# A graph layer's group loop: sums copied by VectorE, carries read from PSUM

## The chip, the cores and the metric

The kernel runs on one core of a Trainium2 chip. A core has five engines with instruction queues of their own: TensorE (matmuls and transposes; PE and PEld in the profile), VectorE (DVE), ScalarE (ACT), GpSimd (POOL) and SyncE (SP). TensorE writes its results to PSUM; the other data on the chip lies in SBUF. The metric is the time of one execution in microseconds (us) on the device; the time given for a kernel is the median of its runs.

## The reference

One layer of graph attention with 12,500 nodes of 128 features and 200,000 edges that are sorted by their destination. It has 4 heads of 32 columns. Cut to what matters:

```python
h = relu(layernorm(x)) @ W_node.T                    # one row for every node
att = leaky(sum([h[src], h[dst], edge @ W_edge.T] * a), 0.2)   # edge x head
m  = max(segment_max(att, dst), 0)                   # node x head
ex = exp(att - m[dst])
den = segment_sum(ex, dst) + (E - degree) * exp(-m)
out = x + segment_sum(ex / den[dst] * h[src], dst)
```

The softmax is taken over all edges, so that the E - degree edges that do not end at a node each add exp(-m) to its denominator.

## The kernel before

**Tiling.** Edges are cut into 392 groups of 511 (`NE`), with one slot ahead of them for a carry, so that a group is 512 slots: 4 columns (`J`) of 128. Four groups are a quad; there are 98 quads. Quads are gathered into super groups of 2, 2, then 4 each, and 2, 2, 1, 1 at the end; a super group shares one softmax. As destinations are sorted, the edges of a group end within a window of 96 nodes (`WIN`), whose first node is a number in the tile `base`.

**Prologue.** GpSimd starts at once to gather the raw rows of the source nodes of quads 0 to 3. Meanwhile TensorE computes a table row of 137 numbers for every node (4 heads of 32 values and a one, a count of one, 4 source terms) and writes it to `table` in HBM. From quad 4 on, GpSimd gathers from `table`: `gather` (L126) issues one indirect DMA of 128 rows for each column, 16 a quad, 1502 in all (L135). The gathered rows of a quad lie in one of eight `ga` buffers. Quads 0 to 3 hold raw rows and are turned into table rows on the core by `converted` (L235); for quads 2 and 3 that is called as `late(2)` and `late(3)` in the main loop, with ScalarE copying from PSUM.

**Main loop.** The order of the work is written out by hand (`tc.manual_schedule()`): every engine runs its instructions in the order in which the program issues them. `together` takes several generators and issues one step of each in turn. In the main loop the generators are these:

- `all_logits(q)` first calls `flush`, which adds up the logits of the quad before it with `add_sources` (L508; L519 is the first to read the gathered rows of that quad). Then it calls for the transfers of quad q + 2, by `fetch`, and computes the logits of its own four groups (L497 on VectorE, L502 and L505 on TensorE).
- `softmax(s)` (L530) transposes the logits of a super group to one row for each group and head, takes the leaky slope (L546 on ScalarE, L549 on VectorE), scans for the maxima of each segment, with what comes in from the group before, and takes exp(att - maximum) (L587). It turns three things back to the layout of edges: the exponentials (L598, in the bank `ex_ps`), a factor for each group's carry (L590, L595, L603, copied to `facs` by L605), and the maximum of each segment, stored at its last edge (L592, L608, copied to `xs` by L610). It has five steps.
- `sums(q)` (L646) prepares the quad: it copies the last-edge flags to column 96 of `hot` (L657) and the maxima to `ga` (L659, one for each group), both on ScalarE. For each group it multiplies the gathered values by the exponentials (L663), makes a one-hot matrix of the destinations (L666) and lets TensorE add up columns 1 to 3 into a PSUM bank `acc` (L671). Then it calls `complete()`, which ends the group before.
- `complete_group` (L627) ends a group. Row 96 of a group's sums is the part of a node that goes on in the next group. VectorE scales it into the carry's slot in column 0 of `ga` (L632), ScalarE copies the count (L636), TensorE adds column 0 (L637), and ScalarE copies the 97 x 137 sums to SBUF, `pt` (L638). After the last group of a quad ScalarE takes exp(-maximum) for the denominators (L642).
- `divide` (L676) divides a quad's sums on VectorE (L681 to L689), adds x (L692), and SyncE writes four windows of 96 rows (L694). Windows overlap, so each write waits for the one before it.

**Buffers and queues.** A `ga` buffer comes free when L637 of the quad's last group has run; GpSimd's gathers of the quad eight later wait for that. The `acc` banks are three in number, and are used by `late` as well. SyncE's queue carries the loads of edge features (`ea`), destinations (`db`), windows of `side` and x (`pw`, `xw`), the destination rows of a super group (`dr`), and the writes. A window's first node is loaded into one of SyncE's registers by `window(g)` (L454), once for `pw` and `xw` and once more for the write. `checked` (L716) tests in small steps, from the sixth super group on, that the destinations are sorted and fit their windows; its four loads of `rows` are issued by ScalarE.

**Main loop's order.** For a super group s of quads q0 and on: the last quad of the super group before is summed in one `together` with the first `all_logits` ahead and `softmax(s)`; then each but the last quad of s is summed beside one `all_logits` of the next super group; then the logits that are left follow. After the first super group, `complete()` and `late(3)` come in between.

Of the kernel before, what the change touches and what calls it, by code (L numbers as in the profile page):

```python
# [8 lines left out]
F32 = mybir.dt.float32  # L9
BF16 = mybir.dt.bfloat16  # L10
I32 = mybir.dt.int32
AF = mybir.ActivationFunctionType
OP = mybir.AluOpType
AX = mybir.AxisListType

P = 128
# [5 lines left out]
LN2 = 0.6931471805599453  # L22

# [3 lines left out]
J = 4  # L27
# [18 lines left out]
def kernel(  # L46
# [388 lines left out]
    with tc.tile_pool(name="work", bufs=2) as work, \  # L435
# [18 lines left out]
        def window(g):  # L454
            return nc.values_load(
                base[0:1, g:g + 1], engines=[mybir.EngineType.SP], min_val=0, max_val=N - 1,
                skip_runtime_bounds_check_because="a destination, which is a node")

        def fetch_windows(q):
# [3 lines left out]
            at = [window(g0 + i) for i in range(m)]  # L463
# [66 lines left out]
        def softmax(s):  # L530
# [14 lines left out]
            low = turned.tile([SBG * H, NE], F32, name="low")  # L545
            nc.scalar.mul(low[:R], t_ps[:R, 1:GE], SLOPE)  # L546
            yield
            att = t_ps[:R, 1:GE]
            nc.vector.tensor_tensor(att, att, low[:R], op=OP.max)  # L549
# [12 lines left out]
            for h in range(H):  # L562
# [13 lines left out]
            top = turned.tile([SBG * H, NE], F32, name="top")  # L576
# [6 lines left out]
                                         op0=OP.mult, op1=OP.max)  # L583
            ex = turned.tile([SBG * H, GE], F32, name="ex")
            nc.vector.memset(ex[:R, 0:1], 0.0)
            nc.vector.tensor_tensor(ex[:R, 1:GE], att, top[:R], op=OP.subtract)
            nc.scalar.activation(ex[:R, 1:GE], ex[:R, 1:GE], AF.Exp)  # L587

            fac = turned.tile([SBG * H, 1], F32, name="fac")
            nc.scalar.activation(fac[:R], top[:R, 0:1], AF.Exp, bias=col[:R], scale=-1.0)  # L590

            nc.vector.scalar_tensor_tensor(run_e, same_next, 0.0, top[:R],  # L592
                                           op0=OP.is_equal, op1=OP.mult)
            diag = turned.tile([SBG * H, SBG * H], F32, name="diag")
            nc.vector.tensor_scalar(diag[:R, :R], ident[:R, :R], fac[:R], None, op0=OP.mult)  # L595
            yield
# [3 lines left out]

            other = acc_pool.tile([P, 512], F32, name="acc")
            fac_ps = other[:, 0:R]
            nc.tensor.matmul(fac_ps, ones[:R, :], diag[:R, :R], start=True, stop=True)  # L603
            facs = turned.tile([P, SBG * H], F32, name="facs", bufs=2)
            nc.scalar.copy(facs[:, :R], fac_ps)  # L605
            top_ps = other[:, 512 - J * SBG * H:].rearrange("p (j r) -> p j r", j=J)[:, :, 0:R]
            for j in range(J):
                nc.tensor.transpose(top_ps[:, j, :], run[:R, j * P:(j + 1) * P], ident[:R, :R])  # L608
            xs = turned.tile([P, J, SBG * H], F32, name="xs", bufs=2)
            nc.scalar.copy(xs[:, :, 0:R], top_ps)  # L610
            XS[s] = ex_ps[:, 0:J * SBG * H].rearrange("p (j r) -> p j r", j=J), xs, facs
# [4 lines left out]
        begun = []  # L616
        state = {}

        def complete():

            division = state.pop("division", None)
            if begun:
                complete_group(*begun.pop())
            if division:
                divide(*division)

        def complete_group(q, i, ga, hot, pt, acc, fc):  # L627
            g0, m = quads[q]
            g = g0 + i
            if g:  # L630
                before = state["before"]
# [4 lines left out]
                nc.scalar.copy(ga[0:1, i, 0, R_CNT:R_CNT + 1], before[WIN:WIN + 1, R_CNT:R_CNT + 1])  # L636
            nc.tensor.matmul(acc, hot[:, i, 0, :], ga[:, i, 0, :], start=False, stop=True)  # L637
            nc.scalar.copy(pt[:, i, :], acc)  # L638
            state["before"] = pt[:, i, :]
            if i == m - 1:  # L640
                den = work.tile([WIN, QG, H], F32, name="den")
                nc.scalar.activation(den[:, :m, :], pt[0:WIN, :m, R_SRC:R_SRC + H], AF.Exp,  # L642
                                     scale=-1.0)
                state["division"] = q, pt, den

        def sums(q):  # L646
# [6 lines left out]
            ex, xs, facs = XS[s]  # L653
# [3 lines left out]
            nc.scalar.copy(hot[:, :m, :, WIN], is_last[:, g0:g0 + m, :])  # L657
            for i in range(m):
                nc.scalar.copy(ga[:, i, :, R_SRC:R_SRC + H], heads(xs)[:, :, :, g0 - s0 + i])  # L659
# [328 lines left out]
```

## Time and profile before

| what | us |
|---|---|
| median of 3 runs | 2074.68 |
| lowest, highest | 2072.62, 2075.88 |
| the profiled execution | 2940.07 |
| its span, first to last instruction | 2938.3 |
| TensorE busy (matmuls) | 1385.1 |
| VectorE busy | 1363.1 |
| ScalarE busy | 427.3 |
| GpSimd busy | 1489.6 |

The profile is of one execution, which took longer than the runs that were timed. Rows of the page and of the answers name a line of the kernel, its engine, its operation and the tiles that it writes and reads; busy time and waits are in us, the mean of one instruction in ns. In a timeline the columns are the start, the duration, the instruction, how many were merged, and in square brackets the idle time of the engine ahead of it with what ended it. "remote" is a wait whose end the profile can't put down to an instruction. The mean granted clock of TensorE was 0.537 of full speed.

### The profile page before, as it was taken

The numbers are of one execution on the slowest core, as the hardware profiler recorded it, in microseconds if no ns is written. First come the engines' busy times: TensorE is split into PE (matmuls) and PEld (weight loads), VectorE is DVE, ScalarE is ACT, GpSimd is POOL, SyncE is SP. The second block draws the span as 40 slices with busy tenths as digits, with TensorE's granted clock in tenths as the row PEclk, the third lists the DMA queues.
The fourth block names the chain that finished last, engine by engine and source line by source line (L and its number), as shares of the span: only waits on it lengthen the run. The fifth ranks groups of instructions, "written<-read, shape, count | busy, mean of one in ns | idle before, by whom it ended". The sixth has DMA issues, their size and how long they took to land.

```text
span 2938.3 us, 29033 instructions
## 1 busy us (share of the span) xinstructions
PE 1385.1 (47%) x7275; PEld 1254.9 (43%) x7275; DVE 1363.1 (46%) x3314; ACT 427.3 (15%) x1766; POOL 1489.6 (51%) x1574
## 2 busy tenths in 40 slices
PE   1524644444445444454454454454454454454465
PEld 1424544444444444444344344344343443444354
DVE  1614444444444444454454454454454454454476
ACT  1523111111111111111111111111111111111111
POOL 7062345555555555555555555555555555555510
PEclk9955555555555555555555555555555555555556
DMA  4333344444444444444444444444444444444320
GB/s 139 124 101 80 85 122 104 100 110 103 100 110 99 110 111 103 99 115 104 99 111 103 102 109 100 106 108 99 106 104 102 109 103 102 110 99 107 92 68 15
DMA packets 214494, 299.10 MB, mean 102 GB/s; under 512 B 86122, under 2 KB 162154, under 8 KB 204915
## 3 DMA queue, kind: packets, MB, share of 16 engines
q1 hardware_dynamic: 162512, 184.97, 23.3%
q0 software_dynamic: 50112, 109.65, 17.3%
q10 hardware_dynamic: 1698, 2.58, 0.3%
q8 instruction: 61, 1.00, 0.1%
q14 instruction: 111, 0.90, 0.1%
HBM read 270.49 MB, written 26.52 MB: 101 GB/s over the span
## 4 chain that ended last, share of the span: by engine, by line
another core or an unknown queue 43%; PE 21%; DVE 14%; issue 10%; ACT 4%; DMA 1%; SPq 1%; ACTq 0%; DVEq 0%
PE acc L671 11%; PE lg L505 4%; PE acc L637 3%; DVE at L497 2%; ACT pt L638 1%; DVE run L575 1%; DVE res L689 1%; DVE res L692 1%; DVE ga L632 1%; DVE hot L666 1%; DVE ga L663 1%; PE lg L502 1%; DVE top L581 1%; PE acc L608 1%
## 5 line engine op out<-in xcount | busy, mean ns | idle before, releaser
L135 POOL DMA_INDIRECT ga<-table,srci x1502 | 1428.1, 951 | 1299.9 <-PE acc L637 774.2
L671 PE MATMUL acc<-ga,hot 128*97 128x137 f32 x2352 | 649.2, 448 | 839.8 <-ACT ga L659 747.4
L671 PEld LDWEIGHTS acc<-ga,hot 128*97 128x97 f32 x2352 | 518.5, 279 | 866.3 <-ACT ga L659 758.0
L632 DVE TENSOR_TENSOR ga<-pt,facs 1x132 f32<-1x132 f32 x391 | 112.6, 288 | 1153.4 <-ACT pt L638 1012.7
L638 ACT COPY pt<-acc 97x137 f32<-97x137 f32 x392 | 107.1, 273 | 2103.2 <-remote 1408.9
L505 PE MATMUL lg<-wblk,ea 128*128 128x8 f32 x1568 | 409.0, 359 | 0.0
L505 PEld LDWEIGHTS lg<-wblk,ea 128*128 128x128 f32 x1568 | 381.5, 309 | 0.0
L637 PE MATMUL acc<-ga,hot 128*97 128x137 f32 x784 | 260.7, 436 | 222.1 <-ACT ga L636 144.8
L502 PEld LDWEIGHTS <-at 96*128 96x128 bf16 x1568 | 218.3, 166 | 206.2 <-DVE at L497 118.2
L637 PEld LDWEIGHTS acc<-ga,hot 128*97 128x97 f32 x784 | 197.2, 283 | 232.3 <-ACT ga L636 150.8
L663 DVE TENSOR_TENSOR ga<-ga,ex_ps 128x528 f32<-128x528 f32 x392 | 270.4, 690 | 9.0 <-PE ex_ps L598 8.6
L497 DVE TENSOR_TENSOR at<-const_ps,db 96x512 bf16<-96x512 f32 x392 | 267.1, 683 | 8.1 <-DMA db<-in_dst_dram 2.3
L502 PE MATMUL lg<-pw,at 96*128 96x12 bf16 x1568 | 169.9, 181 | 141.0 <-DVE at L497 99.6
L666 DVE TENSOR_TENSOR hot<-const_ps,slot 128x384 f32<-128x384 f32 x392 | 214.0, 546 | 0.0
L372 PE MATMUL row_ps<-wcat,hT 128*128 128x137 f32 x198 | 39.9, 351 | 79.6 <-issue 21.4
L598 PE MATMUL ex_ps<-ident,ex 64*128 64x64 f32 (+2 forms) x112 | 18.6, 314 | 123.8 <-ACT ex L587 123.8
L636 ACT COPY ga<-pt 1x1 f32<-1x1 f32 x391 | 73.6, 188 | 10.6
L135 POOL DMA_INDIRECT ga<-in_x_dram,srci x64 | 60.5, 946 | 20.7 <-issue 19.2
L372 PEld LDWEIGHTS row_ps<-wcat,hT 128*128 128x128 f32 x198 | 33.6, 243 | 86.1 <-ACT row L373 23.5
L692 DVE TENSOR_TENSOR res<-res,xw 96x512 f32<-96x512 f32 x98 | 67.7, 691 | 3.4
L689 DVE TENSOR_TENSOR res<-pt,const_ps 96x512 f32<-96x512 f32 x98 | 66.9, 683 | 3.4
L598 PEld LDWEIGHTS ex_ps<-ident,ex 64*128 64x128 f32 (+2 forms) x112 | 13.8, 208 | 126.8 <-ACT ex L587 126.8
(129 smaller groups left out, 1016.0 us busy)
## 6 DMA issues: line engine op xcount, KB each, us to landing
db<-in_dst_dram SPq DMA_DIRECT2D x98, 768.0 KB
ea<-in_edge_t_dram SPq DMA_DIRECT2D x98, 512.0 KB
ga<-table,srci POOLq DMA_INDIRECT x1502
xw<-in_x_dram SPq DMA_DIRECT2D x392, 48.0 KB
out_dram<-res SPq DMA_DIRECT2D x392, 48.0 KB
pw<-side SPq DMA_DIRECT2D x392, 2.2 KB
table<-row SPq DMA_DIRECT2D x9, 616.5 KB
xt<-in_x_dram SPq DMA_DIRECT2D x9, 576.0 KB
```

Of the source, the lines that this page charges most:

```text
L135: nc.gpsimd.indirect_dma_start(out=ga[:, i, j, 0:width], out_offset=None, in_=rows, in_offset=bass.IndirectOffsetOnAxis(ap=srci[:, g0 + i, ...
L497: nc.vector.tensor_tensor(at[:, i, :], node_ps[0:WIN, g0 + i:g0 + i + 1].to_broadcast([WIN, GE]), db[:, i, :], op=OP.is_equal)
L502: nc.tensor.matmul(lg[:, i, j].rearrange("p k h -> p (k h)"), at[:, i, j * P:(j + 1) * P], sw, start=i + j == 0, stop=False, skip_group_ch ...
L505: nc.tensor.matmul(lg[:, i, 2 * w:2 * w + 2, 0, :], ea[:, i, w, :], wblk, start=False, stop=True, skip_group_check=True)
L632: nc.vector.tensor_tensor(ga[0:1, i, 0, 0:H * HW].rearrange("p (h w) -> p h w", w=HW), before[WIN:WIN + 1, 0:H * HW].rearrange("p (h w) -> ...
L637: nc.tensor.matmul(acc, hot[:, i, 0, :], ga[:, i, 0, :], start=False, stop=True)
L638: nc.scalar.copy(pt[:, i, :], acc)
L663: nc.vector.tensor_tensor(val, val, heads(ex)[:, :, :, g - s0].unsqueeze(3).to_broadcast([P, J, H, HW]), op=OP.mult)
L666: nc.vector.tensor_tensor(hot[:, i, :, 0:WIN], lane_ps.unsqueeze(1).to_broadcast([P, J, WIN]), slot[:, g, :].unsqueeze(2).to_broadcast([P, ...
L671: nc.tensor.matmul(acc, hot[:, i, j, :], ga[:, i, j, :], start=j == 1, stop=False)
L689: nc.vector.tensor_tensor(res[:, :m, :].rearrange("p g (h d) -> p g h d", d=HD), val[:, :, :, 0:HD], share_ps[:, :m, :].unsqueeze(3).to_br ...
L692: nc.vector.tensor_tensor(res[:, :m, :], res[:, :m, :], xw[:, :m, 0:D], op=OP.add)
```

## The change

It takes ScalarE's copies out of the group loop:

- The bank `acc` of a group is copied to `pt` by VectorE, and one `complete()` later than before: a new list `full` holds the group whose sums are in the bank and not yet copied. The carry of the next group is read from that bank, both its values and its count, by VectorE.
- The last-edge flags and the maxima are copied by VectorE, the maxima of all four groups in one instruction, out of PSUM.
- The leaky slope is taken by VectorE.
- In the softmax ScalarE takes exp(-maximum) for every edge ahead of the last-edge mask, so that the sums hold it at each node and the division needs no exp of its own. A node without edges gives zero there, and `TINY` keeps its denominator from being zero. The carry's factor is taken by the first exp as element 0 of `ex`. The softmax has six steps, and its results stay in the `ex_ps` bank.
- SyncE loads the first nodes of four windows by one call in place of four.
- The four loads of `rows` are issued by SyncE, and the end of the kernel calls `complete()` three times.

```diff
-        def window(g):
-            return nc.values_load(
-                base[0:1, g:g + 1], engines=[mybir.EngineType.SP], min_val=0, max_val=N - 1,
+        def windows(q):
+            g0, m = quads[q]
+            return nc.values_load_multi_w_load_instructions(
+                base[0:1, g0:g0 + m], engines=[mybir.EngineType.SP], min_val=0, max_val=N - 1,
...
-            low = turned.tile([SBG * H, NE], F32, name="low")
-            nc.scalar.mul(low[:R], t_ps[:R, 1:GE], SLOPE)
             yield
             att = t_ps[:R, 1:GE]
-            nc.vector.tensor_tensor(att, att, low[:R], op=OP.max)
+            top = turned.tile([SBG * H, NE], F32, name="top")
+            nc.vector.tensor_scalar(top[:R], att, SLOPE, None, op0=OP.mult)
+            nc.vector.tensor_tensor(att, att, top[:R], op=OP.max)
...
-            nc.vector.memset(ex[:R, 0:1], 0.0)
             nc.vector.tensor_tensor(ex[:R, 1:GE], att, top[:R], op=OP.subtract)
-            nc.scalar.activation(ex[:R, 1:GE], ex[:R, 1:GE], AF.Exp)
-            fac = turned.tile([SBG * H, 1], F32, name="fac")
-            nc.scalar.activation(fac[:R], top[:R, 0:1], AF.Exp, bias=col[:R], scale=-1.0)
+            nc.vector.tensor_tensor(ex[:R, 0:1], col[:R], top[:R, 0:1], op=OP.subtract)
+            nc.scalar.activation(ex[:R], ex[:R], AF.Exp)
+            nc.scalar.activation(top[:R], top[:R], AF.Exp, scale=-1.0)
+            yield
+            diag = turned.tile([SBG * H, SBG * H], F32, name="diag")
+            nc.vector.tensor_scalar(diag[:R, :R], ident[:R, :R], ex[:R, 0:1], None, op0=OP.mult)
             nc.vector.scalar_tensor_tensor(run_e, same_next, 0.0, top[:R],
                                            op0=OP.is_equal, op1=OP.mult)
-            diag = turned.tile([SBG * H, SBG * H], F32, name="diag")
-            nc.vector.tensor_scalar(diag[:R, :R], ident[:R, :R], fac[:R], None, op0=OP.mult)
-            yield
             for j in range(J):
                 nc.tensor.transpose(ex_ps[:, j * SBG * H:j * SBG * H + R], ex[:R, j * P:(j + 1) * P],
                                     ident[:R, :R])
-            other = acc_pool.tile([P, 512], F32, name="acc")
             fac_ps = other[:, 0:R]
             nc.tensor.matmul(fac_ps, ones[:R, :], diag[:R, :R], start=True, stop=True)
-            facs = turned.tile([P, SBG * H], F32, name="facs", bufs=2)
-            nc.scalar.copy(facs[:, :R], fac_ps)
-            top_ps = other[:, 512 - J * SBG * H:].rearrange("p (j r) -> p j r", j=J)[:, :, 0:R]
+            yield
+            facs = turned.tile([WIN + 1, SBG * H], F32, name="facs", bufs=2)
+            nc.vector.tensor_copy(facs[WIN:WIN + 1, :R], fac_ps[WIN:WIN + 1, :])
+            top_ps = other.rearrange("p (j r) -> p j r", j=J)[:, :, 0:R]
             for j in range(J):
                 nc.tensor.transpose(top_ps[:, j, :], run[:R, j * P:(j + 1) * P], ident[:R, :R])
-            xs = turned.tile([P, J, SBG * H], F32, name="xs", bufs=2)
-            nc.scalar.copy(xs[:, :, 0:R], top_ps)
...
         def complete():
             division = state.pop("division", None)
+            ready = full.pop() if full else None
             if begun:
-                complete_group(*begun.pop())
+                complete_group(ready[-1] if ready else state.get("before"), *begun.pop())
+            if ready:
+                q, i, pt, acc = ready
+                nc.vector.tensor_copy(pt[:, i, :], acc)
+                state["before"] = pt[:, i, :]
+                if i == quads[q][1] - 1:
+                    state["division"] = q, pt
             if division:
                 divide(*division)
-        def complete_group(q, i, ga, hot, pt, acc, fc):
+        def complete_group(before, q, i, ga, hot, pt, acc, fc):
...
-                nc.scalar.copy(ga[0:1, i, 0, R_CNT:R_CNT + 1], before[WIN:WIN + 1, R_CNT:R_CNT + 1])
+                nc.vector.tensor_copy(ga[0:1, i, 0, R_CNT:R_CNT + 1],
+                                      before[WIN:WIN + 1, R_CNT:R_CNT + 1])
             nc.tensor.matmul(acc, hot[:, i, 0, :], ga[:, i, 0, :], start=False, stop=True)
-            nc.scalar.copy(pt[:, i, :], acc)
-            state["before"] = pt[:, i, :]
-            if i == m - 1:
-                den = work.tile([WIN, QG, H], F32, name="den")
-                nc.scalar.activation(den[:, :m, :], pt[0:WIN, :m, R_SRC:R_SRC + H], AF.Exp,
-                                     scale=-1.0)
-                state["division"] = q, pt, den
+            full.append((q, i, pt, acc))
...
-            nc.scalar.copy(hot[:, :m, :, WIN], is_last[:, g0:g0 + m, :])
-            for i in range(m):
-                nc.scalar.copy(ga[:, i, :, R_SRC:R_SRC + H], heads(xs)[:, :, :, g0 - s0 + i])
+            nc.vector.tensor_copy(hot[:, :m, :, WIN], is_last[:, g0:g0 + m, :])
+            nc.vector.tensor_copy(
+                ga[:, :m, :, R_SRC:R_SRC + H],
+                heads(tops_at)[:, :, :, g0 - s0:g0 - s0 + m].rearrange("p j h g -> p g j h"))
...
-            nc.vector.tensor_tensor(den[:, :m, :], den[:, :m, :],
+            nc.vector.tensor_tensor(den[:, :m, :], pt[0:WIN, :m, R_SRC:R_SRC + H],
                                     others[:, :m].unsqueeze(2).to_broadcast([WIN, m, H]), op=OP.mult)
-            nc.vector.tensor_tensor(den[:, :m, :], den[:, :m, :], val[:, :, :, HD], op=OP.add)
+            nc.vector.scalar_tensor_tensor(den[:, :m, :], val[:, :, :, HD], TINY, den[:, :m, :],
+                                           op0=OP.max, op1=OP.add)
...
-                nc.scalar.dma_start(rows[:n], dst_rows[g0:g0 + n, 0:NE + 1])
+                nc.sync.dma_start(rows[:n], dst_rows[g0:g0 + n, 0:NE + 1])
...
-            complete()
-            complete()
+            for _ in range(3):
+                complete()
```

## The prediction

> **What bounds the kernel now.** I read the page first, then the table of waits, GpSimd's timeline, the timeline of one standstill, and the tail. The page, engines, chain and costliest group:
>
> ```profile
> PE 1385.1 (47%) x7275; PEld 1254.9 (43%) x7275; DVE 1363.1 (46%) x3314; ACT 427.3 (15%) x1766; POOL 1489.6 (51%) x1574
> another core or an unknown queue 43%; PE 21%; DVE 14%; issue 10%; ACT 4%; DMA 1%; SPq 1%; ACTq 0%; DVEq 0%
> L135 POOL DMA_INDIRECT ga<-table,srci x1502 | 1428.1, 951 | 1299.9 <-PE acc L637 774.2
> ```
>
> No engine is full, and 43% of the chain has no name. The waits (us in total, times, longest) put it on ScalarE's copy of the sums:
>
> ```profile
> ACT pt L638 <- remote: 1408.9, 102, 19.1
> DVE ga L632 <- ACT pt L638: 1012.7, 160, 14.6
> POOL ga L135 <- PE acc L637: 774.2, 85, 63.9
> POOL ga L135 <- issue: 449.3, 1473, 0.6
> ```
>
> It looks as if ScalarE held the loop. The timeline of one such wait (start, us, instruction) says otherwise:
>
> ```profile
> 1539.72 0.57 PE L505 MATMUL lg<-wblk,ea 128*128 128x8 f32 x2
> 1539.91 0.94 POOL L135 DMA_INDIRECT ga<-table,srci  x1 [0.30 <-issue]
> ...
> 1552.59 0.27 ACT L638 COPY pt<-acc 97x137 f32<-97x137 f32 x1 [15.64 <-remote]
> ```
>
> The matmul that L638 needs began at 1538.68, yet TensorE, VectorE and ScalarE all stand still for 12.3 us; only GpSimd goes on. Summing in the timeline the stretches over 1.5 us with none of the three at work gives 124 standstills, 1107 us. The profiled execution took 2940.07 us (span 2938.3, 1.8 around it), the median run 2074.68: 865 us less, which only these standstills can supply. I take them for the recording's. Without them the engines need 2938.3 - 1107 = 1831 us, and GpSimd is what remains:
>
> ```profile
> 161.13 0.94 POOL L135 DMA_INDIRECT ga<-table,srci  x1 [78.32 <-DMA table<-row]
> ...
> 304.66 0.94 POOL L135 DMA_INDIRECT ga<-table,srci  x1 [63.94 <-PE acc L637]
> ...
> 350.23 0.94 POOL L135 DMA_INDIRECT ga<-table,srci  x1 [25.89 <-PE acc L637]
> ...
> 385.92 0.94 POOL L135 DMA_INDIRECT ga<-table,srci  x1 [15.87 <-PE acc L637]
> 421.64 0.94 POOL L135 DMA_INDIRECT ga<-table,srci  x1 [16.07 <-PE acc L637]
> ```
>
> Gathers start 1.256 us apart (mean of 1474 unbroken steps, stops left out), so 16, a quad, take 20.1 us. These rows show gathers of quads 8 to 11 waiting until quads 0 to 3 give back their buffers. Standstills before the five rows sum to 44, 110, 119, 131 and 142 us; taken out, the table is ready at 117.0 and the buffers free at 195.2, 231.0, 254.5 and 279.8. GpSimd would reach them at 197, 217, 251 and 275: it waits 14 + 4 + 5 us, last at quad 3. From there 1502 - 64 - 48 = 1390 gathers x 1.256 = 1746 lead to 2025.6. Then the tail:
>
> ```profile
> 2894.64 0.27 DVE L519 TENSOR_TENSOR U<-st,ga 128x64 f32<-128x64 f32 x1
> ...
> 2925.55 0.69 DVE L692 TENSOR_TENSOR res<-res,xw 96x512 f32<-96x512 f32 x1
> ```
>
> L519 is the first to need the last gather; from it to the end are 43.7 us without a standstill. 2025.6 + 43.7 + 1.8 = 2071.1; the median is 3.6 more (a landing's latency is left out). So the run is paced by GpSimd, except up to quad 3's release and in the tail, where VectorE and TensorE decide.
>
> [...] the windows show 0.50 from 1640 to 1750 us. [...] 73 gathers take over 1.0 us instead of 0.94, and 62 of them overlap L692, which reads two SBUF tiles; none overlaps L681, an SBUF-to-SBUF operation with one input like the new `hot` copy. So I give the new copies no effect on the gathers.
>
> **The change, part by part.** *Group loop.* Per quad ScalarE loses 4 L638 (273 ns), 4 L636 (188), L657 (220), 4 L659 (214) and L642 (218): 3.1 us. VectorE gets 4 bank copies, 4 count copies, one `hot` and one maxima copy. Its PSUM copies of 512 and 384 columns take 689 and 550 ns, 1.09 ns a column, so 137 columns cost 0.28 and 64 cost 0.21; a one-column copy (L574) 0.147; small SBUF copies (L561, L566) 0.15 to 0.22, I take 0.18. Quad: 4 x 0.43 + 0.18 + 0.21 = 2.1 us. *Softmax.* The slope becomes a 511-column VectorE operation on PSUM, 0.68 as L549; `facs` 0.15; a memset of 0.06 goes: 0.77 per super group. Its end grows a round: diag waits for the first exp, run for the second, facs for the matmul, the top transposes for both, and the maxima copy, ahead of L663, for them. Followed through the super group at 1523.8, L663 starts 1.7 us later and L671 0.8 later. *Carry.* TensorE to VectorE directly: about 0.3 us off a hop that already lies beside 2.9 us of matmuls a group. L632 now waits on TensorE in VectorE's own queue; behind it stand the bank copy, the division and the next L497, which TensorE's L502 needs. It waited at that place before, for L638. *Banks.* An `acc` is copied a group later: when a new one is taken two are in use, of three, so the loop adds no wait.
>
> The new second exp on ScalarE (0.63, as L587) is seen only in that 1.7. In the steady loop all this is hidden by GpSimd's 20.1 us. Quads take 13.6 us without standstills (26.0 - 12.3), those with a softmax 24.4; mean 16.3. Adding 2.1 + 0.77/4 + 1.7/4 gives 19.0: hidden, with 1.1 to spare; gone, it would cost 98 x the excess.
>
> On the path:
> - Release of quad 0: slope 0.1 (0.68 for 0.58) and the softmax end 0.8: 0.9. The group steps there are TensorE's.
> - `late(3)`: the last sums of quad 0 now stay in their bank until after it, so its transposes and matmuls turn over two of three `acc` banks. Bounds 0 and 5 (eight row copies at 0.39 and four at 0.58 made serial); I take 2.5.
> - To quad 1: VectorE is busy 21.9 of 45.5 - 9.7 us, 12 of which are late(3): full. Added before the softmax's end: one bank copy, then a count, then two groups of 0.43, the maxima copy 0.21, slope less memset 0.62: 2.1; with 0.8: 2.9.
> - To quad 2: 15.1 of 23.5 busy: 0.7. To quad 3: 20.4 of 25.3, again a softmax: 1.72 + 0.39 + 0.62 + 0.8 = 3.5.
> - Sum: 10.5 us, passed on whole, as GpSimd already waits there.
> - Tail: VectorE works 25.0 of 32.3 us. It gains nine bank and eight count copies (3.7), slope, facs, hot and maxima (1.2) and loses waits of 0.6, 1.6, 1.0, 1.2 and 0.9 partly; followed row by row, the last division starts 1.4 (softmax) + 1.7 later: 3.1.
>
> *SyncE.* Six of eight register loads a quad go (0.31 us apart, 1.9 us); SyncE waits anyway. Taken at 0; VectorE waited 2.3 us for `db` before quad 3, so -2.3 at best. Its out-writes wait 1.5 to 2.4 us for one another; the loads lay inside that. *The four `rows` DMAs* now queue behind SyncE's wait for L497 (longest 16 us); their reader comes a quad later: 0, at worst four waits of that length, which the eight quads of gather buffers absorb. *TINY* swaps one operation for another: 0.
>
> Sum: 2074.7 + 10.5 + 3.1 = 2088.3; L632 no longer reads two SBUF tiles (ten slow gathers lie beside it, 0.16 each: -1.6). I forecast **2087 us**.
>
> **Rivals.** (A, 58%) As above, 2079 to 2096. (B, 20%) Hidden anyway: the start is held by TensorE's half clock and ScalarE's conversions, so the added VectorE work fits their gaps, and only the tail's 3 us show: 2077. For it: VectorE is idle for the 12 us of late(3). Against: full in the softmax stretches. (C, 10%) VectorE becomes the bound: if the standstills also hid waits and a quad needs 20.6 us, 90 quads x 0.5 = 45 us: 2120, more beyond. For it: 19.0 is near 20.1. [...] (D, 12%, faster) The carry and ScalarE's queue hold back the first releases: L657 waited behind late(3)'s conversions until 326.3. If the freed hops shorten the way to quad 3 by more than the added 10.5, GpSimd's waits of 23 us shrink; with half of them gone, less the tail's 3: 2066. The floor, no wait of GpSimd's left, is 2074.7 - 23 = 2052.
>
> **How the numbers follow.** Less than 0.2% (4 us) is about what a measurement cannot tell from no change. A gives slower 53, same 5; B same 15, slower 5; C slower 10; D faster 11, same 1. Faster 0.11, same 0.21, slower 0.68. Range 2068 to 2104: it leaves out D's lower half and most of C. A's own range is 2079 to 2096.
>
> **What would show it.** Gathers still 1.25 us apart; no ACT row in the group loop; bank copies on VectorE near 0.28, slope 0.68; from the last L519-type addition (`U` from `st`) to the end 46 to 48 us; releases of quads 1 and 3 later by 3 to 6 us each, standstills taken out. Its span is no measure: standstills may shift. I am wrong if the standstills are in the timed runs too, when the carry's hop decides and it becomes faster, or if a quad needs over 20.1 us of VectorE.

## The result and the profile after

| | before | after |
|---|---|---|
| median (runs) | 2073.89 us (4) | 2088.84 us (4) |
| lowest, highest | 2072.62, 2075.88 | 2088.21, 2091.39 |
| profiled execution, span | 2070.82, 2068.9 (second profile) | 2088.72, 2086.8 |

The ratio is 1.0074, with a 95% interval of 1.0056 to 1.0091: slower by some 15 us. The forecast was 2087.

One thing is needed to read the numbers below: in the last three of the sets of runs, each on a chip of its own, every kernel took 2.85 to 2.94 ms, timed runs included, and stood still in its trace about once a quad as in the first profile of before, so kernels are compared only within a set. The kernel before was profiled a second time (the experiment before_again), in a set without standstills; that trace is the one compared with here.

The page of the kernel after: engines, then the gathers' and the first reader's groups (busy time, mean ns, then idle time of the engine ahead of them and its end).

```profile
PE 1367.9 (66%) x7275; PEld 1239.8 (59%) x7275; DVE 1563.0 (75%) x4349; ACT 134.4 (6%) x311; POOL 1497.2 (72%) x1574
L136 POOL DMA_INDIRECT ga<-table,srci x1502 | 1435.2, 956 | 490.6 <-issue 471.1
L521 DVE TENSOR_TENSOR U<-st,ga 128x64 f32<-128x64 f32 x98 | 26.2, 268 | 336.5 <-DMA ga<-table,srci 335.1
```

The same of the second profile of before, with its chain:

```profile
PE 1373.7 (66%) x7275; PEld 1249.3 (60%) x7275; DVE 1364.4 (66%) x3314; ACT 426.7 (21%) x1766; POOL 1503.4 (73%) x1574
POOL 47%; issue 20%; DVE 17%; DMA 6%; PE 5%; ACT 2%; SPq 1%; DVEq 0%; POOLq 0%; ACTq 0%
L135 POOL DMA_INDIRECT ga<-table,srci x1502 | 1441.4, 960 | 479.4 <-issue 445.0
```

ScalarE lost two thirds of its work and VectorE gained 199 us. The chain of before, which had 43% without a name in the first profile, is now GpSimd's gathers and the 0.3 us of issue between them, 67% together. For the kernel after, the profile follows that chain over 1% of the span only; there the sign is that VectorE waits 335 us for gathers that have not landed: GpSimd still sets the pace.

The places where GpSimd waits, in GpSimd's timeline of the kernel after (start, us, instruction, idle time ahead):

```profile
92.84 0.94 POOL L136 DMA_INDIRECT ga<-table,srci  x1 [9.37 <-DMA table<-row]
...
201.68 0.94 POOL L136 DMA_INDIRECT ga<-table,srci  x1 [8.41 <-issue]
...
225.95 0.95 POOL L136 DMA_INDIRECT ga<-table,srci  x1 [4.59 <-issue]
...
257.40 0.94 POOL L136 DMA_INDIRECT ga<-table,srci  x1 [11.68 <-issue]
...
2008.30 0.94 POOL L136 DMA_INDIRECT ga<-table,srci  x1 [0.30 <-issue]
```

and of before, second profile:

```profile
94.77 0.94 POOL L135 DMA_INDIRECT ga<-table,srci  x1 [11.59 <-DMA table<-row]
...
218.27 0.94 POOL L135 DMA_INDIRECT ga<-table,srci  x1 [3.41 <-PE acc L637]
...
246.12 0.94 POOL L135 DMA_INDIRECT ga<-table,srci  x1 [7.53 <-PE acc L637]
...
2003.09 0.94 POOL L135 DMA_INDIRECT ga<-table,srci  x1 [0.30 <-issue]
```

After the first row, a row with a long wait is a gather that waits for a buffer of quad 1, 2 or 3, and starts 2.9 to 3.7 us after that quad's last carry (so also in the trace of after, whose rows name no releaser); after the last of these GpSimd runs without a stop to its last gather (the last row). So an execution falls into three parts, and the 17.9 us between the two spans into three differences:

| part | before | after | difference | forecast |
|---|---|---|---|---|
| start, to the last such wait | 246.1 | 257.4 | +11.3 | +10.5 |
| 1389 steps to the last gather | 1757.0 (1.2649 each) | 1750.9 (1.2605 each) | -6.1 | -1.6 |
| last gather to the end | 65.8 | 78.5 | +12.7 | +3.1 |
| span | 2068.9 | 2086.8 | +17.9 | +12.0 |

### The profile page after: what moved, and what is told of

It reads as the page before. It is cut to its first block, busy times and chain, and to the rows that moved or that the text cites. A ratio compares the mean times of both kernels' runs of the same rounds, so it can differ in the third digit from the quotient of the medians.

```text
span 2086.8 us, 27038 instructions
## 1 busy us (share of the span) xinstructions
PE 1367.9 (66%) x7275; PEld 1239.8 (59%) x7275; DVE 1563.0 (75%) x4349; ACT 134.4 (6%) x311; POOL 1497.2 (72%) x1574
## 5 line engine op out<-in xcount | busy, mean ns | idle before, releaser
L504 PEld LDWEIGHTS <-at 96*128 96x128 bf16 x1568 | 211.4, 164 | 526.6 <-DVE at L499 502.1
L521 DVE TENSOR_TENSOR U<-st,ga 128x64 f32<-128x64 f32 x98 | 26.2, 268 | 336.5 <-DMA ga<-table,srci 335.1
L499 DVE TENSOR_TENSOR at<-const_ps,db 96x512 bf16<-96x512 f32 x392 | 267.2, 683 | 12.0 <-DMA db<-in_dst_dram 8.0
L663 DVE TENSOR_TENSOR hot<-const_ps,slot 128x384 f32<-128x384 f32 x392 | 213.9, 546 | 0.0
L589 ACT ACTIVATE ex<-ex 64x512 f32<-64x512 f32 (+2 forms) x28 | 17.6, 629 | 1856.6 <-DVE ex L588 1856.6
L633 DVE TENSOR_TENSOR ga<-acc,facs 1x132 f32<-1x132 f32 x390 | 115.6, 296 | 16.6 <-PE acc L639 4.7
L624 DVE COPY pt<-acc 97x137 f32<-97x137 f32 x392 | 117.8, 301 | 12.7 <-PE acc L639 0.5
L692 DVE TENSOR_TENSOR res<-res,xw 96x512 f32<-96x512 f32 x98 | 67.5, 689 | 3.4
L637 DVE COPY ga<-acc 1x1 f32<-1x1 f32 x390 | 58.4, 150 | 0.0
```

Of the source, the lines that this page charges most:

```text
L499: nc.vector.tensor_tensor(at[:, i, :], node_ps[0:WIN, g0 + i:g0 + i + 1].to_broadcast([WIN, GE]), db[:, i, :], op=OP.is_equal)
L504: nc.tensor.matmul(lg[:, i, j].rearrange("p k h -> p (k h)"), at[:, i, j * P:(j + 1) * P], sw, start=i + j == 0, stop=False, skip_group_ch ...
L624: nc.vector.tensor_copy(pt[:, i, :], acc)
L633: nc.vector.tensor_tensor(ga[0:1, i, 0, 0:H * HW].rearrange("p (h w) -> p h w", w=HW), before[WIN:WIN + 1, 0:H * HW].rearrange("p (h w) -> ...
L663: nc.vector.tensor_tensor(hot[:, i, :, 0:WIN], lane_ps.unsqueeze(1).to_broadcast([P, J, WIN]), slot[:, g, :].unsqueeze(2).to_broadcast([P, ...
L692: nc.vector.tensor_tensor(res[:, :m, :], res[:, :m, :], xw[:, :m, 0:D], op=OP.add)
```

## The experiments

**A second profile of before, and parts of the change.** before_again is the kernel before. softmax_only undoes the group loop:

```diff
-            ready = full.pop() if full else None
             if begun:
-                complete_group(ready[-1] if ready else state.get("before"), *begun.pop())
-            if ready:
...
+                complete_group(state.get("before"), *begun.pop())
...
-                nc.vector.tensor_copy(ga[0:1, i, 0, R_CNT:R_CNT + 1],
...
+                nc.scalar.copy(ga[0:1, i, 0, R_CNT:R_CNT + 1],
...
-            full.append((q, i, pt, acc))
+            nc.scalar.copy(pt[:, i, :], acc)
...
-            nc.vector.tensor_copy(hot[:, :m, :, WIN], is_last[:, g0:g0 + m, :])
...
+            nc.scalar.copy(hot[:, :m, :, WIN], is_last[:, g0:g0 + m, :])
+            for i in range(m):
+                nc.scalar.copy(ga[:, i, :, R_SRC:R_SRC + H], heads(tops_at)[:, :, :, g0 - s0 + i])
```

group_only keeps the group loop and undoes the softmax's arithmetic:

```diff
+            nc.scalar.mul(low[:R], t_ps[:R, 1:GE], SLOPE)
...
-            nc.vector.tensor_scalar(top[:R], att, SLOPE, None, op0=OP.mult)
...
-            nc.scalar.activation(ex[:R], ex[:R], AF.Exp)
...
-            nc.scalar.activation(top[:R], top[:R], AF.Exp, scale=-1.0)
...
+            nc.scalar.activation(ex[:R, 1:GE], ex[:R, 1:GE], AF.Exp)
...
+            nc.scalar.activation(fac[:R], top[:R, 0:1], AF.Exp, bias=col[:R], scale=-1.0)
...
-            nc.vector.tensor_copy(facs[WIN:WIN + 1, :R], fac_ps[WIN:WIN + 1, :])
...
+            nc.scalar.copy(facs[:, :R], fac_ps)
...
+            nc.scalar.copy(xs[:, :, 0:R], top_ps)
```

and extra_complete empties the bank that stays held over `late(3)`:

```diff
                 if not s:
                     complete()
+                    complete()
                     together(*late(3))
```

Expected of before_again:

> The kernel before, unchanged, for a second profile. Theory (recorder's standstills): the time stays at 2072 to 2076, and where no standstill falls the trace shows GpSimd's stops directly. By the sum of the prediction its last stop, the release of quad 3, ends about 10.5 us earlier than the 257.4 us of the changed kernel, at 247, and the last gather starts at about 247 + 1390 x 1.257 = 1994 (changed kernel: 2008.3). Rival (the start is not where the time went): quad 3 is released at 255 or later, and the difference of 15 us lies after the last gather and in the pace of the gathers (1.2605 us after, 1.2569 before: 5 us).

Of softmax_only:

> The changed kernel with the group loop as before: sums, count, flags and maxima copied by ScalarE, the sums in the same group. Kept of the change: the softmax (slope on VectorE, both exps, factors, six steps), the division without exp, and SyncE's loads. Theory (the sum of the prediction): of the 10.5 + 3.1 us the softmax brings 0.9 + 1.4 + 1.4 at the releases of quads 0, 1 and 3 and some 2 in the tail, 5 to 6 us: 2079 to 2080. Rival (the start does not count, the tail does): 2076 or less. Rival (the softmax's longer end is all of it): 2086 or more.

Of group_only:

> The changed kernel with the softmax's arithmetic as before (slope, one exp an edge, factors and maxima copied by ScalarE, exp for the denominators on ScalarE after the sums' copy), its results still in the ex_ps bank. Kept of the change: sums copied by VectorE a group later, carry and count from the bank, flags and maxima by VectorE, SyncE's loads. Theory (the sum of the prediction): late(3) with a held bank 2.5, groups 1.5 + 0.7 + 2.1 at the releases, 1.7 in the tail: 8 to 9 us, 2082 to 2083. Rival (the carry from the bank is a gain and the softmax the loss): 2074 or less.

Of extra_complete:

> The changed kernel with one more complete() ahead of late(3), so that the last sums of quad 0 leave their bank first and late(3) has all three. Theory (the sum of the prediction took 2.5 us for late(3) with two banks): 2.5 us less than the changed kernel, 2086.3, and the release of quad 1 as much earlier than 201.7. If the held bank costs nothing: 2088.8 and 201.7. If it is the upper bound: 2083.8.

Measured, all in one set, beside a median of 2072.99 us for the kernel before (parts read from each trace as above, us):

| kernel | time | ratio (95%) | first table gather | start | pace | tail |
|---|---|---|---|---|---|---|
| before_again | 2070.82 | - | 94.8 | 246.1 | 1.2649 | 65.8 |
| softmax_only | 2099.53 | 1.0131 (1.0116 to 1.0147) | 95.7 | 251.7 | 1.2702 | 79.5 |
| group_only | 2080.76 | 1.0040 (1.0025 to 1.0056) | 92.5 | 255.5 | 1.2557 | 77.2 |
| extra_complete | 2087.84 | 1.0065 (1.0052 to 1.0079) | 94.3 | 257.2 | 1.2601 | 80.1 |
| after | 2088.84 | 1.0074 (other set) | 92.8 | 257.4 | 1.2605 | 78.5 |

before_again was to be released at 247, and was at 246.1: the start is where the forecast had put it. Its last gather came at 2003.1, not 1994, since its own gathers are slower, 1.2649 us, than the 1.257 of the first profile.

softmax_only is 26.5 us slower (start +5.6, pace +7.4, tail +13.6), more than the whole change and far from the 5 to 6 us of the theory; only the bound of the last rival takes it in, and for another reason than its length. Its waits name what is new in it (us in total, times, longest):

```profile
DVE ga L655 <- ACT ga L651: 196.7, 96, 2.7
```

This is a wait that neither whole kernel has. The changed softmax leaves the maxima in the bank `ex_ps`, beside the exponentials, and here it is ScalarE that copies them from there. VectorE's first multiplication of a quad, which reads the same bank, waits 2.0 us for these copies in 96 of 98 quads, those without a softmax of their own included. In the kernel before, ScalarE copies the maxima from SBUF (`xs`), and that multiplication waits for no copy of ScalarE's; in the kernel after, VectorE copies them itself and waits 15.4 us in all, for TensorE. In the middle of softmax_only GpSimd's pace hides the waits, but eight of them, 15.3 us, lie between the first readers of quads 92 and 97, where the tail grew; the 7.4 us of the pace are in long gathers (below). So the run does not price the softmax alone.

group_only came within 2 us of its expectation of 8 to 9 us, but by cancellation: with a longer start and tail (+9.4, +11.4) and a gain of 12.8 in the pace that the expectation did not have. Nor is it free of the softmax's longer end. From VectorE's subtraction ahead of the exp (L586 of the kernel before) to the next group sums of TensorE it is 4.25 us in the kernel before (median of 28), 5.12 in the kernel after, 5.38 in group_only, where VectorE's copy of the maxima waits for ScalarE's `xs`, and 5.62 in softmax_only. Both halves pay for it, so their costs do not add up to that of the change.

extra_complete: against the changed kernel's 35.9 us between the last carries of quads 0 and 1 (162.9 to 198.8), it takes 34.6 (164.1 to 198.7). By this the held bank costs 1.3 us, not 2.5. The release of quad 1, which the expectation had named, stayed where it was (201.6 beside 201.7), since quad 0's last carry came 1.2 us later in this trace, and the time, 1.0 us lower, is not clear of noise: with one trace of each, 1.3 is an estimate.

**The tail.** The two traces tell where its time went. In the kernel before, the first reader of quad 92's gathers (L519; L521 after) is the last that waits for its gathers; in the kernel after, quad 91's is. From quad 92's reader to quad 97's the windows show, for before (second profile):

```profile
core 0: us, PE busy (x) PEld busy (x) DVE busy (x) ACT busy (x) POOL busy (x), PEclk, DMA share, GB/s
1907.50:2025.60 118.10, 90.99 (x465) 82.63 (x463) 100.81 (x236) 27.02 (x124) 73.64 (x76) 0.51 0.40 101
```

and for after:

```profile
1916.80:2045.20 128.40, 86.90 (x472) 77.45 (x471) 117.90 (x321) 3.44 (x6) 70.19 (x74) 0.61 0.38 92
```

VectorE is busy 85% of the stretch before and 92% after: 17.1 us more, of which 6.8 go into its old gaps (17.3 us free before, 10.5 after) and 10.3 lengthen the stretch. Most of the old gaps, 11.2 us, are waits for ScalarE's copy, in the groups of VectorE in that stretch of before (us 1907 to 2026):

```profile
L632 DVE TENSOR_TENSOR ga<-pt,facs 1x132 f32<-1x132 f32 x32 | 9.3, 290 | 11.8 <-ACT pt L638 11.2
```

and the new work, in those of after (1916 to 2046):

```profile
L624 DVE COPY pt<-acc 97x137 f32<-97x137 f32 x33 | 9.9, 301 | 1.0
L633 DVE TENSOR_TENSOR ga<-acc,facs 1x132 f32<-1x132 f32 x33 | 9.8, 297 | 2.0 <-PE acc L639 1.0
L637 DVE COPY ga<-acc 1x1 f32<-1x1 f32 x33 | 4.9, 150 | 0.0
L654 DVE COPY ga<-ex_ps 128x64 f32<-128x64 f32 x8 | 1.7, 218 | 1.4 <-PE ex_ps L607 1.4
L653 DVE CAST hot<-is_last 128x16 f32<-128x16 bf16 x8 | 1.7, 212 | 0.1
```

Another 4.1 us lie ahead of the stretch (the reader of quad 92 comes 7.0 us after that quad's last gather, 3.7 before; the rest is the pace of the last gathers), 1.5 from the last reader to the last addition of x, and from there to the end it is 3.3 shorter: 10.33 + 4.09 + 1.54 - 3.27 = 12.7.

**SyncE, and the two ends, tried in sets with standstills.** sync_undone takes SyncE's part back:

```diff
...
-            at = windows(q)
             for i in range(m):
-                nc.sync.dma_start(out[bass.ds(at[i], WIN), :], res[:, i, :])
+                nc.sync.dma_start(out[bass.ds(window(g0 + i), WIN), :], res[:, i, :])
...
-                nc.sync.dma_start(rows[:n], dst_rows[g0:g0 + n, 0:NE + 1])
+                nc.scalar.dma_start(rows[:n], dst_rows[g0:g0 + n, 0:NE + 1])
```

ends_as_before is group_only with VectorE's copies only in the middle, where GpSimd sets the pace:

```diff
+        def on_scalar(q):
+            return q < 4 or q >= 88
...
-            full.append((q, i, pt, acc))
+            if on_scalar(q):
+                nc.scalar.copy(pt[:, i, :], acc)
+                state["before"] = pt[:, i, :]
+                if i == quads[q][1] - 1:
+                    divisor(q, pt)
+            else:
+                full.append((q, i, pt, acc))
```

no_residual leaves the addition of x (L692) out of the changed kernel, and hot_twice issues its one-hot matrix (L663) twice in quads 12 to 87:

```diff
-            nc.vector.tensor_tensor(res[:, :m, :], res[:, :m, :], xw[:, :m, 0:D], op=OP.add)
```

```diff
-                nc.vector.tensor_tensor(
-                    hot[:, i, :, 0:WIN], lane_ps.unsqueeze(1).to_broadcast([P, J, WIN]),
+                for _ in range(2 if 12 <= q < 88 else 1):
+                    nc.vector.tensor_tensor(
+                        hot[:, i, :, 0:WIN], lane_ps.unsqueeze(1).to_broadcast([P, J, WIN]),
```

Of sync_undone:

> The changed kernel with SyncE's part undone: a register load for each window and each write, and the four loads of rows issued by ScalarE. Theory (the prediction took this part at 0): 2088.8 within 4 us. Rival (the loads of rows in SyncE's queue, or the loads of four registers, move the tail or the start): the tail after the last gather, 78.5 us in the changed kernel, or the release of quad 3, 257.4 us, differs by more than 3 us.

Of ends_as_before:

> group_only with its group loop only for quads 4 to 87; quads 0 to 3 and 88 to 97 have ScalarE's copies as before, the softmax is as before throughout. Theory (the loss lies at the two ends, where VectorE sets the pace, and the gathers' pace is a gain of fewer SBUF reads by VectorE): quad 3 is released at 246 as in the kernel before, the gathers keep about 1.2557 us as in group_only, and the tail is 66 us as before: 246.1 + 1389 x 1.2557 + 66 + 1.9 = 2058, faster than both. Rival (the ends do not matter, the middle does): 2077 or more, like group_only (2080.8).

Of no_residual:

> The changed kernel without the addition of x to the result (L692), which is left out of the computation. Theory (a gather that starts while VectorE reads two SBUF tiles is held up): the 33 slow gathers at L692, 12.6 us together from the 176th gather on, go; pace from 1.2605 to about 1.2515. With 3 + 9 such additions of 0.69 us less in the start and the tail, some 2 + 5 us: 2088.8 - 12.6 - 7 = 2069. Rival (slow gathers are the memory's): pace unchanged at 1.2605, 2082.

Of hot_twice:

> The changed kernel with L663 (the one-hot matrix, 0.55 us) issued twice in every group of quads 12 to 87: 2.2 us more of VectorE a quad, about as much again as the change added, only where the gathers set the pace. Theory of the prediction (19.0 of 20.1 us used, 1.1 to spare): 76 x 1.1 = 84 us slower, 2172. Reading of the new trace (VectorE waits 335 us for gathers, some 4 us a quad in these 76): hidden, 2089 within 5 us, the lag of the logits' addition behind the gathers a little longer. Rival (VectorE sets the pace in the middle too): 76 x 2.2 = 167 us slower, 2256.

The set had standstills, and so had two more, in which three of these kernels were run again (ends_as_before twice). Of the second and third run of ends_as_before:

> The kernel of ends_as_before once more: in the set in which it ran first every kernel, the one before too (2888.8 us), stood still as the first profile of before did. Theory (the loss lies at the two ends, VectorE setting the pace there): without standstills 2058, faster than both; quad 3 released at 246, tail 66 us. Rival (the ends do not matter, the middle does): 2077 or more. If the standstills are there again: 2866 and a ratio of 0.993, as in that set.

> The kernel of ends_as_before for a set without standstills. Theory (the loss lies at the two ends, VectorE setting the pace there): quad 3 released about 151 us after the first gather from the table, as in the kernel before (246.1 - 94.8), a tail of 66 us or, with the shorter last writes, 63; gathers at 1.2557 to 1.2605: 2055 to 2065, faster than both. Rival (the ends do not matter, the middle does): 2077 or more. If all kernels of the set stand still again, a ratio of 0.989 to 0.993, as in the sets before.

Of the second run of no_residual:

> The changed kernel without the addition of x to the result (L692), left out of the computation, for a set without standstills. Theory (a gather that starts while VectorE reads two SBUF tiles is held up): pace from 1.2605 to about 1.2515, 12.6 us, and 0.69 us for each such addition in the start and the tail, 5 to 7 us: 2069 to 2072. Rival (slow gathers are the memory's): pace 1.2605, 2082. With standstills: about 0.989 of the kernel before.

Of the second run of hot_twice:

> The changed kernel with L663 twice in quads 12 to 87, 2.2 us of VectorE more a quad, for a set without standstills. Theory of the prediction (1.1 us a quad to spare): 76 x 1.1 = 84 us slower than the changed kernel, 2172. Reading of the new trace (VectorE waits 334.8 us for gathers between quad 3's release and quad 92, 4.2 us a quad): hidden, 2089 within 8 us, the pace of the gathers apart, and those waits fall to some 2 us a quad. Rival (VectorE paces the middle): 2256. With standstills: as the changed kernel without its register loads, about 0.996 of the kernel before.

| set (before, us) | sync_undone | ends_as_before | no_residual | hot_twice |
|---|---|---|---|---|
| 2888.80 | 2876.05, 0.9961 (0.9945 to 0.9977) | 2866.37, 0.9928 (0.9905 to 0.9951) | 2856.70, 0.9894 (0.9863 to 0.9924) | 2880.08, 0.9965 (0.9951 to 0.9978) |
| 2936.97 | | 2903.32, 0.9894 (0.9872 to 0.9916) | | |
| 2934.41 | | 2905.22, 0.9892 (0.9876 to 0.9909) | 2890.22, 0.9839 (0.9819 to 0.9859) | 2922.85, 0.9972 (0.9958 to 0.9987) |

The absolute numbers expected without standstills could not be tested. The waits of sync_undone show what such an execution looks like:

```profile
DVE ga L632 <- remote: 788.2, 111, 12.5
POOL ga L136 <- PE acc L638: 595.9, 83, 15.6
```

The carry, which reads TensorE's bank, waits up to 12.5 us for it about once a quad, and GpSimd in turn for its buffers; GpSimd no longer sets the pace. What can be read all the same:

- SyncE's part is not nothing. From the last addition of x to the end the kernel before takes 12.3 us, sync_undone 11.4, the changed kernel 9.05, and every other kernel here that has its loads and adds x 9.0 to 9.3. SyncE's timeline has the last four writes, from the first to the end of the last, for before (second profile) and for after:

```profile
2057.34 6.23 SPq L694 DMA_DIRECT2D out_dram<-res  x4
```

```profile
2078.51 4.89 SPq L695 DMA_DIRECT2D out_dram<-res  x4
```

The register loads themselves are not what shows: with a load between them or without, each of these writes is issued 0.02 us after the one before it has landed. From the first of the four to the last it is 5.90 and 4.57 us, as the first two land later in the trace of before. The other 2.0 us are a pause of SyncE behind the last write, among its closing waits (us in total, times, longest), here for before (second profile), sync_undone and after:

```profile
SPq L792 <- SPq L792: 2.5, 2, 2.0
```

```profile
SPq L791 <- SPq L791: 2.6, 2, 2.1
```

```profile
SPq L793 <- SPq L793: 0.5, 1, 0.5
```

It is there in all three traces with a load for every window (the first of before too) and in none of the others; what SyncE waits for in it they do not show.

- ends_as_before is 9.7 us under sync_undone in one set. In the traces its wait for quad 3's buffer ends at 413.8 against 418.5 and its tail is 129.8 against 137.7 (2.3 of this lie behind the last addition of x), while the gathers between take 4.1 longer. That fits a cost at the ends, but the softmax as before and SyncE's loads set the two apart as well, and these runs do not separate them: it is not shown. ends_as_before is faster than the kernel before in all three sets, by 22 to 34 us. Whether it is without standstills stays open.
- Twice the one-hot work in 76 quads, 4 x 0.55 us each or 167 us, leaves hot_twice at 2880 beside 2876 for sync_undone: hidden, but there among waits for TensorE, as the 788 us of sync_undone above.
- no_residual cannot test the long gathers: with the gathers stopping in every quad only 13 gathers of sync_undone take over 1.0 us, and 6 of no_residual. Its 19 us beside sync_undone are not split further.

## Why the prediction was right, and where it was not

**The bound: right.** The second profile of before shows it directly, GpSimd's gathers with their issue are 67% of the chain. **The baseline was right by cancellation.** The prediction built 2071.1 from a release at 279.8, a pace of 1.256 and a tail of 43.7; the second trace has 246.1, 1.2649 and 65.8, and 1757.0 for the gathers where it had 1746, that is -33.7, +11.2 and +22.1. Taking standstills out of a trace gave the sum, not the places.

**The standstills are the recording's: fell.** before_again, a recorded execution of 2070.82 us, is without the 12 us standstills of the first profile, and the timed runs of three sets take as long as the traces with them (2852 to 2940 us). That the recording makes them was the author's estimate, from the 865 us between the first profiled execution and the median run; no run here shows it. The number did not hang on it, since the timed runs shown were free of standstills. The prediction said that with standstills in the timed runs the carry's hop would decide and the change be faster; in those sets the kernel nearest to the change, sync_undone, has a ratio of 0.9961. What the standstills are, these runs do not settle: a wait for TensorE's results in the traces (1408.9 us in 102 waits in the first profile of before, 788.2 in 111 in sync_undone), at a mean granted clock of TensorE of 0.52 to 0.54 with them (the prediction's 0.50 from 1640 to 1750 us is this clock, in the first profile) and 0.53 to 0.54 without. The set without them ran on one chip and the three sets with them on three others, so the chip is a rival that no run here tests.

**The start: right in place, and nearly in size.** The last carry of quads 0 to 3 (L632, L633) starts at 161.5, 191.7, 214.9 and 242.8 before and at 162.9, 198.8, 222.3 and 254.5 after: steps of 1.4, 5.7, 0.3 and 4.3 us, where the sum had 0.9, 5.4, 0.7 and 3.5. In the second step the term for `late(3)`, 2.5, was too large (1.3) and the rest, 2.9, too small (4.4). The softmax's end was right: 0.9 us later (4.25 and 5.12, above) for 0.8. GpSimd's waits were not: the prediction had 14 + 4 + 5 us at quads 1, 2 and 3, the second profile of before has none at quad 1, 3.4 at quad 2 and 7.5 at quad 3. The delay still passes on, as it is quad 3's release that GpSimd meets last. Counted from the first table gather, which came 1.9 us earlier in the trace of after (and between 92.5 and 95.7 us in the five), the start is 13.2 longer in place of 10.5.

**The pace: right in direction, too small.** The gathers are 6.1 us faster, not 1.6. By the VectorE instruction that runs as a long gather starts, the time that such gathers take over 0.946 us is, from the 176th on: before, 7.4 at L581, 4.6 at L539, 3.4 at L692, 2.8 at L592 and 2.4 at the carry L632; after, 13.1 at L692, 1.6 at L541 and 0.8 at L499. The carry's share is gone as forecast. Summed over all gathers of this stretch, not the long ones alone, the time over 0.946 us stands beside the time of the 1389 steps as follows:

| us | before_again | softmax_only | group_only | extra_complete | after |
|---|---|---|---|---|---|
| over 0.946 us, in all | 21.8 | 29.3 | 10.3 | 15.3 | 16.0 |
| 1389 steps | 1757.0 | 1764.4 | 1744.1 | 1750.3 | 1750.9 |

The two move together, and the time between one gather and the next sums to 423 us in each: the pace differs by how long the gathers themselves take, and that mostly by the long ones. The part beyond the carry's share moved with the phase, it seems: in steady work VectorE waits for the gathers, so a quad's instructions meet the same gather again and again. Of the gathers over 1.0 us that start in L692 behind quad 3's release, all 61 in the first profile start 0.40 to 0.42 us into it, and 26 of the 33 in the trace of after 0.08 to 0.11. One such meeting, in the timeline of after:

```profile
1216.40 0.94 POOL L136 DMA_INDIRECT ga<-table,srci  x1 [0.30 <-issue]
...
1217.55 0.69 DVE L692 TENSOR_TENSOR res<-res,xw 96x512 f32<-96x512 f32 x1
1217.65 1.40 POOL L136 DMA_INDIRECT ga<-table,srci  x1 [0.30 <-issue]
```

The gather starts 0.1 us into the addition, which reads two SBUF tiles, and takes 1.40 us in place of 0.94; in the first profile it came 0.4 us into it and took 1.10. The prediction's count, 62 of 73 slow gathers over L692, points the same way. That it is the two inputs is argued from where the long gathers start, though from many of them (see the last section); the run that was to show it fell to standstills.

**The tail: the step that failed.** The sum let the tail begin at L519 of the last quad, as the first to need the last gather. It does not wait: it comes 22.5 us (36.9 after) behind that gather's start. The last reader near its gather is quad 92's (3.7 us behind it, 7.0 after), and from there on, over the last, smaller super groups, VectorE sets the pace, with eight quads' sums up to the last reader of which none was counted. The unit costs were right: the bank copy measured 0.30 (0.28 taken), the count 0.15 (0.147), `hot` 0.22 (0.18), the maxima 0.22 (0.21), the slope 0.67 (0.68). Eight times 2.1 and three softmaxes of 0.77 make 19.1 us (17.1 measured), less the 6.8 that VectorE's gaps took in 12.3, for a stretch that grew by 10.3. Behind the last reader 3.1 was forecast and 1.5 measured up to the addition of x, and **SyncE at 0** failed too: the end behind that addition gave back 3.3, though not by the register loads, which lay inside the waits as the prediction had said. So the 46 to 48 us named as a sign came out as 41.6. The other signs held: gathers 1.25 us apart, no row of ScalarE in the group loop, copies and slope as priced, releases of quads 1 and 3 later by 5.7 and 4.3 more each.

**Hidden in the middle: right, with more to spare.** Between the last release and quad 92 the waits for gathers are, before (second profile, 246 to 1907) and after (257 to 1917):

```profile
DVE U L519 <- DMA ga<-table,srci: 435.5, 76, 11.6
```

```profile
DVE U L521 <- DMA ga<-table,srci: 334.8, 59, 8.6
```

Over some 83 quads in each stretch that is 5.2 us of slack a quad before and 4.0 after, not 1.1. VectorE's busy time in the stretch grew from 1073.7 to 1241.5 us, and GpSimd's did not grow with it (columns as in the windows of the tail):

```profile
246.00:1907.00 1661.00, 1094.49 (x5752) 998.79 (x5753) 1073.67 (x2451) 274.02 (x1281) 1260.69 (x1314) 0.51 0.57 145
```

```profile
257.00:1917.00 1660.00, 1090.66 (x5750) 994.04 (x5751) 1241.46 (x3336) 24.13 (x42) 1258.56 (x1317) 0.51 0.62 145
```

So 2087 beside 2088.84 owes some of its closeness to luck: start +0.8, pace -4.5 and tail +9.6 make the traces' 17.9 out of the forecast's 12.0, and the medians, over more runs, lie 15.0 apart. **Rivals.** A holds. B (hidden start) falls with +11.3 (TensorE's granted clock was 0.59 from 92 to 246 us before, second profile, and 0.56 from 92 to 257 after), C (VectorE paces the middle) with the waits above, D (earlier releases) with last carries later by 1.4 to 11.7; its floor of 2052 also rested on 23 us of GpSimd's waits, of which the second profile has 11.

## What to carry to other kernels

Here one engine paced the steady loop, and the work moved onto another cost nothing there (VectorE busy 167.8 us more in a stretch of 1660 us beside 1661) and its price at the two ends (11.3 and 12.7 us). Where a loop is paced like this, find in the trace the last reader that still waits for the pacing engine, and price the change from there to the end, not from the last item. A run of a part of a change is not always the price of that part: softmax_only cost more than the whole, with a wait of 2.0 us a quad that neither whole kernel has. Look for such a wait in its trace before reading its time. And look at the end behind the last result as well: a part that was priced at 0 gave back 3.3 us there.

## What the runs showed of the hardware

- Indirect gathers that started 0.06 us or more into a VectorE instruction with two SBUF inputs (L692, L541, L632) were longer the more was left of it, in the first profile of before and the trace of after: 0.94 or 0.95 us with up to 0.12 us left, 1.02 to 1.04 with 0.20 to 0.22, 1.08 to 1.11 with 0.27 to 0.29, 1.40 to 1.43 with 0.58 to 0.61. Behind quad 3's release, 342 of the 347 gathers over 1.0 us in five kernels start in an instruction that reads two inputs or more from SBUF (scans, comparisons, the addition of x, the carry from `pt`). Of the 6373 that start elsewhere 5 are over 1.0 us (the three of after start in L499 while L541 or L740, with two SBUF inputs, runs already or begins up to 0.47 us later), and none of the 445 of before_again that start in L497, L663 or L666, which have one input in PSUM. The pace lay between 1.2557 and 1.2702 us in the five kernels, 20 us of the run.
- The same kernel took 2070 to 2077 us in one set, on one chip, and 2880 to 2940 in three others, on three other chips, at the same mean granted clock (0.53 to 0.54, and 0.52 to 0.54), with standstills of some 12 us about once a quad in the traces.
- Of SyncE's last four writes, each is issued 0.02 us after the one before it has landed, most of them 1.5 us after their own issue. A register load of 0.27 us between two of them lay inside that wait: the last two are issued 1.52 us apart with it (first profile of before) and 1.53 without (after).
